# Four slot tiles of the two attention layers are summed in PSUM, in two places chosen by a number, behind a branch

## The chip, the core and the metric

The kernel runs on one core of one Trainium2 chip. The metric is device time in microseconds (us), from one launch; the median of the runs is compared. Engines are called PE (matrix multiply), DVE (vector), ACT (scalar), POOL (gpsimd) and SP (sync). POOL here does little but issue indirect DMAs, which gather table rows by a list of indices; SP issues the plain DMAs.

## What is computed

A stack of four graph layers over 3,125 nodes of 256 features and 50,000 edges, each followed by a residual and a layer norm. Edges come sorted by their destination `dst`; their density falls with the node number (`dst` is 3125 times a squared uniform number), so the first nodes have many edges and the last have few. Layers 1 and 2 are the ones that the change touches. Both are attention over the edges into a node:

```python
# layer 1: H = 4 heads of 64; layer 2: H = 8 heads of 64
score = <key of source, query of destination>        # layer 1
score = leaky(s_src[src] + s_tgt[dst])               # layer 2
m     = segment_max(score, dst);  ex = exp(score - m[dst])
out   = segment_sum(ex * value[src], dst) / segment_sum(ex, dst)
x     = layernorm(x + f(out))
```

Layer 0 is an edge-weighted mean with a gate, layer 3 a relational convolution. They are not changed.

## The kernel before

**Slot tiles.** Nodes are cut into 25 node tiles of 128. The sorted edges are cut into slot tiles of up to 128 edges that all go to one node tile; there are 416 (`TT`), so a node tile has between about 5 and 80 consecutive slot tiles. The number of the node tile of each slot tile is computed on the chip in `bucket` and kept in `tnode` (L333); engines read it into registers with `node_of` (L534), which loads four numbers at a time (L523).

**The edge loop** (`edge_softmax`, L714) goes over 26 steps of 16 slot tiles (`S`), each step four groups of four (`G`). For a group, `score` (L1228 in layer 1, L1390 in layer 2) has POOL gather four tiles of 128 table rows (2 KB a row; L509) into one of seven buffers `gb`, has SP load the one-hot matrices `oh` and `oht` (L548), multiplies on PE the transposed one-hots by the destination's query (`pqe`, L1237) or by its score part (`pst`, L1398), and reduces to scores on DVE (L1242, L1243; L1403 to L1405). When the 16 tiles have scores, `softmax` (L607 to L680) runs a chain of small operations that switches between PE, DVE and ACT and ends in the weights `ex` (L666).

**`weigh`** (L682) then adds the weighted values of a group into the accumulator `acc`, which holds all 25 node tiles in SBUF. It multiplies the gathered values by `ex` into `r`: DVE does all but `on_act` of the heads in one instruction (L697), ACT does the last `on_act` heads with one instruction per head and slot tile (L701). `on_act` is 2 in layer 1 and 3 in layer 2. Then, for each of the four slot tiles, PE multiplies `r` by the one-hot (L706: one 128x260 float32 matmul in layer 1, two in layer 2) into a PSUM tile `pr` of its own, and DVE adds that tile to the place in `acc` that the tile's node number names (L711):

```python
for j in range(G):
    pr = ps.tile([P, H // HB, 512], F32, name="pr", bufs=3)
    for n in range(H // HB):
        nc.tensor.matmul(pr[:, n, :HB * F], oh[:, j, :], r[:, j, n*HB:(n+1)*HB, :], start=True, stop=True)
    node = self.node_of(nc.vector, t0 + j)
    a = acc[:, ds(node * (H * F), H * F)]
    nc.vector.tensor_add(a, a, pr[:, :, :HB * F])
```

A gather buffer is free again when both DVE's and ACT's part of `r` are made. The scores of a step and the weighing of the step before it are interleaved; each engine's order of instructions is fixed when the program is built, by a scheduler that sees the whole program, and each engine runs its own list in order.

**Around the edge loops.** Layer 1's loop stands between the making of its tables (L1194 and the puts of L501) and a finishing stage (L1252 on) that scales `acc`, applies a typed matmul and prepares layer 2's tables. The scheduler puts parts of the neighbours into the loops' ends: weights of the finishing stage (`al` L1253, `wh` L1328) are loaded, `al` is scaled (L1258) and the vectors `wa` are made (L1336, L1337) while layer 1's last groups are still added up. The memsets of layer 2's accumulator (L1384) run beside its first gathers. There is one branch in the kernel, at L280: a sort that is skipped when the edges come sorted.

Of the kernel before, what the change touches and what calls it, by code (L numbers as in the profile page):

```python
# [9 lines left out]
F32 = mybir.dt.float32  # L10
# [10 lines left out]
G = 4  # L21
# [12 lines left out]
class Net:  # L34
# [4 lines left out]
    def __init__(self, ctx, tc, n_nodes, n_edges):  # L39
# [19 lines left out]
        self.below = c.tile([P, P], F32, name="below")  # L59
        nc.vector.tensor_scalar(self.below, self.iota, self.pidx, None, op0=ALU.is_gt)  # L60
# [152 lines left out]
    def bucket(self, src, dst, type16, type8, weight, relations):  # L213
# [27 lines left out]

        with tc.tile_pool(name="bk", bufs=1, side="right") as b:
# [40 lines left out]
            with tc.tile_pool(name="bkw", bufs=1, side="right") as w, tc.tile_pool(name="bkp", bufs=1, space=PSUM) as ps:  # L283
# [49 lines left out]
                nc.vector.tensor_copy(self.tnode, tno[0:1, :])  # L333
                p = pick(lambda k: bdf[:, k, :], "pdst")
# [202 lines left out]

    def used(self, engine, inst):
        self.uses.setdefault(engine.engine, []).append(inst.ins)
# [142 lines left out]
    def weigh(self, w, ps, acc, ohb, ex, value, H, t0, on_act):  # L682
# [19 lines left out]
        yield  # L702
        for j in range(G):
# [10 lines left out]
    def edge_softmax(self, w, sm, ps, hand, acc, H, F, score, on_act):  # L714
# [3 lines left out]
        def done(steps):  # L718
            for _ in steps:
                pass  # L720
# [3 lines left out]
        for t0 in range(0, self.TT + S, S):  # L724
# [8 lines left out]
            for n in range(S // G):  # L733
                if not last:
                    held.append(score(t0 + n * G, sc[:, :, n * G:(n + 1) * G]))
                if before and (last or n < S // G - 1):
                    value, oh = before[n]
                    done(self.weigh(w, ps, acc, oh, ex, value, H, t0 - S + n * G, on_act))
# [3 lines left out]
            if before:  # L742
                value, oh = before[-1]
                rest = self.weigh(w, ps, acc, oh, ex, value, H, t0 - G, on_act)
# [360 lines left out]
    def layer1(self, k_lin, q_lin, v_lin, a_lin, rel_att, rel_msg, rel_pri, skip,  # L1105
# [13 lines left out]
        with ExitStack() as layer:  # L1119
# [6 lines left out]
            with ExitStack() as edges:  # L1126
# [98 lines left out]
                with tc.tile_pool(name="e1g", bufs=7) as gp, tc.tile_pool(name="e1", bufs=2) as w, \  # L1225
                        tc.tile_pool(name="e1o", bufs=4) as op, tc.tile_pool(name="e1s", bufs=3) as sm, \
                        tc.tile_pool(name="e1p", bufs=2, space=PSUM) as ps:
                    def score(g0, out):  # L1228
                        gb = gp.tile([P, G, 2 * D], F32, name="gb1")
                        for j in range(G):  # L1230
                            self.gather(gb[:, j, :], table, self.s_rel, g0 + j)
                        oh, oht = self.onehots_back(w, op, g0)
                        pq = ps.tile([P, G, D], F32, name="pqe", bufs=2)
                        for j in range(G):
                            node = self.node_of(nc.tensor, g0 + j)
                            for n in range(3):
                                last = nc.tensor.matmul(pq[:, j, :], oht[:, j, :],  # L1237
                                                        q_all[:, ds(node * (3 * D) + n * D, D)],
                                                        start=n == 0, stop=n == 2)
                            self.used(nc.tensor, last)  # L1240
                        pd = w.tile([P, G, D], F32, name="pd")
                        nc.vector.tensor_mul(pd, gb[:, :, 0:D], pq)  # L1242
                        nc.vector.tensor_reduce(out.rearrange("p h t -> p t h"),  # L1243
                                                pd.rearrange("p j (h d) -> p j h d", h=H),
                                                axis=AX.X, op=ALU.add)
                        return gb[:, :, D:], oh

                    self.edge_softmax(w, sm, ps, hand, acc, H, F, score, 2)
# [125 lines left out]
    def layer2(self, Wo, bo, nxt):  # L1374
# [5 lines left out]
        with ExitStack() as layer:  # L1380
# [6 lines left out]
            with tc.tile_pool(name="e2g", bufs=7) as gp, tc.tile_pool(name="e2", bufs=2) as w, \  # L1387
                    tc.tile_pool(name="e2o", bufs=4) as op, tc.tile_pool(name="e2s", bufs=3) as sm, \
                    tc.tile_pool(name="e2p", bufs=2, space=PSUM) as ps:
                def score(g0, out):  # L1390
                    gb = gp.tile([P, G, HO + H], F32, name="gb2")
                    for j in range(G):
                        self.gather(gb[:, j, :], table, self.s_src, g0 + j)
                    oh, oht = self.onehots_back(w, op, g0)
                    pst = ps.tile([P, G, 3, H], F32, name="pst", bufs=1)
                    for j in range(G):
                        node = self.node_of(nc.tensor, g0 + j)
                        last = nc.tensor.matmul(pst[:, j, :, :], oht[:, j, :], s_tgt[:, ds(node * (3 * H), 3 * H)],  # L1398
                                                start=True, stop=True)
                        self.used(nc.tensor, last)  # L1400

                    pl = sm.tile([P, G, H], F32, name="pl")
                    nc.vector.tensor_reduce(pl, pst.rearrange("p j n h -> p j h n"), axis=AX.X, op=ALU.add)  # L1403
                    nc.vector.tensor_add(pl, pl, gb[:, :, HO:])
# [220 lines left out]
```

## Time and profile before

| what | us |
|---|---|
| median of 3 runs | 3369.55 (3362.56 to 3373.93) |
| the profiled execution's own time | 3362.08 |
| its span, first to last instruction | 3360.3 |
| layer 1's edge loop with its tail, 1168 to 1806 us of the span | 638 |
| layer 2's edge loop with its tail, 1968 to 2661 us of the span | 693 |

In the whole span PE is busy 80%, DVE 68%, POOL 54%, ACT 43%; in the two edge loops the shares differ, and they are read there. In the rows "busy, mean ns" is the time of a group of like instructions and the mean of one; "idle before, releaser" is how long the engine had stood still just before them, and who ended that. A float32 matmul is two passes in the records, so L706 counts two for each matmul. "issue" is time in which an engine waited for nothing that the profile shows. Rows that end in q (POOLq, DVEq, PEldq) are an engine's sequencer: branches, register loads, semaphores.

### The profile page before, as it was taken

What the parts mean: (1) busy time and instruction counts of PE and PEld (TensorE: products, weight loads), DVE (VectorE), ACT (ScalarE), POOL (GpSimd) and SP (SyncE); (2) the same over time, 40 slices, a digit from 0 to 9 for tenths busy, and PEclk for the clock granted to TensorE, in tenths of its full rate; (3) what the DMA queues carried; (4) which work ended last, traced back from release to release, by engine and by line L of the source; (5) the groups of instructions that cost most, each with busy time, mean ns of one, the idle gap of its engine ahead of it and who ended that gap; (6) DMA issues with size and microseconds to landing.
All of it is one profiled execution on the core that took longest, in us unless ns stands there. A gap on an engine that the chain in (4) does not pass through costs nothing. (4 is left out here: it accounts for less than half of the span.)

```text
span 3360.3 us, 50557 instructions
## 1 busy us (share of the span) xinstructions
PE 2693.6 (80%) x12679; PEld 1753.9 (52%) x12679; DVE 2274.4 (68%) x6046; ACT 1446.9 (43%) x4376; POOL 1827.1 (54%) x1850
## 2 busy tenths in 40 slices
PE   2779999999979777777775847888888887888885
PEld 1357777775545345555553525666666663333332
DVE  2646666676655378988886437888888873555556
ACT  1427777774456335544543215656656562000000
POOL 4037767771044167666662556676766202777773
PEclk9889999999989878888887878888888985565656
DMA  7249988884067877777774367878777235333332
GB/s 167 72 147 295 295 284 289 287 291 137 32 252 288 311 225 244 232 230 238 228 229 136 116 206 201 225 225 227 228 226 228 76 140 215 105 105 106 106 105 86
DMA packets 240616, 658.40 MB, mean 196 GB/s; under 512 B 47960, under 2 KB 87012, under 8 KB 234013
## 3 DMA queue, kind: packets, MB, share of 16 engines
q0 software_dynamic: 132400, 484.37, 46.4%
q1 hardware_dynamic: 104262, 167.53, 15.1%
q10 hardware_dynamic: 3676, 3.23, 0.5%
q8 instruction: 122, 2.00, 0.2%
q14 instruction: 156, 1.28, 0.1%
HBM read 513.06 MB, written 151.58 MB: 198 GB/s over the span
## 5 line engine op out<-in xcount | busy, mean ns | idle before, releaser
L509 POOL DMA_INDIRECT gb<-table,s_src x832 | 852.4, 1025 | 374.8 <-issue 203.9
L706 PE MATMUL pr<-r,oh 128*128 128x260 f32 x2496 | 733.6, 440 | 80.7 <-DVE acc L711 32.9
L706 PEld LDWEIGHTS pr<-r,oh 128*128 128x128 f32 x2496 | 502.5, 217 | 216.0 <-issue 33.1
L1509 POOL DMA_INDIRECT ring<-table,b_rel x391 | 369.9, 946 | 312.8 <-DVE oh L1519 194.0
L701 ACT ACTIVATE r<-gb,ex 128x64 f32<-128x64 f32 x2080 | 522.4, 336 | 0.0
L509 POOL DMA_INDIRECT gb<-table,s_rel x416 | 405.4, 974 | 204.9 <-issue 106.0
L711 DVE TENSOR_TENSOR acc<-acc,pr 128x260 f32 (+1 forms) x832 | 457.7, 550 | 72.7 <-PE pr L706 60.8
L1538 PE MATMUL pa<-ring,oh 128*128 x832 | 428.9, 628 | 84.1 <-DMA ring<-table,b_rel 41.2
L1538 PEld LDWEIGHTS pa<-ring,oh 128*128 128x128 f32 x832 | 193.7, 283 | 319.6 <-DVE oh L1519 215.2
L1545 DVE TENSOR_TENSOR x<-x,pa 128x256 f32 x416 | 175.2, 421 | 227.0 <-PE pa L1538 225.2
L1237 PE MATMUL pqe<-q_all,oht 128*128 x1248 | 207.8, 306 | 91.9 <-DVE pd L1242 76.1
L693 ACT CAST oh<-ohb 128x512 f32<-128x512 bf16 x208 | 128.3, 618 | 307.2 <-PE pr L706 278.6
L589 ACT ACTIVATE r<-mv,eps 128x4 f32<-128x4 f32 (+3 forms) x27 | 7.9, 297 | 536.5 <-DVE mv L575 533.1
L697 DVE TENSOR_TENSOR r<-gb,ex 128x512 f32<-128x512 f32 (+1 forms) x208 | 225.8, 1086 | 12.9 <-ACT ex L666 9.2
L979 PE MATMUL pa<-gb,ohw 128*128 128x272 f32 x832 | 223.7, 402 | 5.3 <-DVE acc L981 3.8
L1237 PEld LDWEIGHTS <-oht 128*128 128x128 bf16 x1248 | 131.6, 107 | 126.8 <-issue 86.0
L961 PE MATMUL pre<-xb,oht 128*128 x1248 | 193.7, 273 | 0.0
L981 DVE TENSOR_TENSOR acc<-acc,pa 128x272 f32 x416 | 180.7, 434 | 6.2 <-PE pa L979 3.4
L928 DVE TENSOR_TENSOR places<-iota,s_dl 128x512 bf16<-128x512 f32 x104 | 72.0, 692 | 161.5 <-ACT ohw L976 161.5
L956 PE MATMUL pre<-gb,idb 128*128 128x512 bf16 x624 | 169.3, 381 | 5.3 <-DMA gb<-table,s_src 5.3
L979 PEld LDWEIGHTS pa<-gb,ohw 128*128 128x128 f32 x832 | 141.5, 190 | 55.6 <-issue 35.1
L967 DVE SCALAR_TENSOR_TENSOR hg<-hg,aw 128x256 f32<-128x256 f32 x416 | 159.4, 421 | 16.1 <-ACT hg L965 16.1
(381 smaller groups left out, 4291.6 us busy)
## 6 DMA issues: line engine op xcount, KB each, us to landing
ohb<-oh_d SPq DMA_DIRECT2D x104, 256.0 KB
oht<-oht_d SPq DMA_DIRECT2D x104, 256.0 KB
table<-row SPq DMA_DIRECT2D x25, 1024.0 KB
gb<-table,s_src POOLq DMA_INDIRECT x832, 4.5
oh_d<-places SPq DMA_DIRECT2D x52, 256.0 KB
oht_d<-oht SPq DMA_DIRECT2D x52, 256.0 KB
sgm<-seg SPq DMA_DIRECT2D x26, 320.0 KB
gb<-table,s_rel POOLq DMA_INDIRECT x416, 4.4
```

What stands on the lines that cost most here:

```text
L509: self.nc.gpsimd.indirect_dma_start(out=out, out_offset=None, in_=table, in_offset=bass.IndirectOffsetOnAxis(ap=idx[:, t:t + 1], axis=0))
L697: nc.vector.tensor_mul(r[:, :, :nd, :hw], v[:, :, :nd, :], ex[:, :nd, s0:s0 + G].rearrange("p h t -> p t h")[:, :, :, None].to_broadcast([ ...
L701: nc.scalar.activation(r[:, j, h, :hw], v[:, j, h, :], AF.Copy, scale=ex[:, h, s0 + j:s0 + j + 1])
L706: nc.tensor.matmul(pr[:, n, :HB * F], oh[:, j, :], r[:, j, n * HB:(n + 1) * HB, :].rearrange("p h f -> p (h f)"), start=True, stop=True)
L711: self.used(nc.vector, nc.vector.tensor_add(a, a, pr[:, :, :HB * F]))
L961: last = nc.tensor.matmul(q, oht[:, 0, j, :], xbr[:, ds(node * (3 * D) + n * D, D)], start=False, stop=False)
L979: nc.tensor.matmul(pa, ohw[:, j, :], gb[:, j, 0:ET + D], start=True, stop=True)
L981: self.used(nc.vector, nc.vector.tensor_add(a, a, pa))
L1237: last = nc.tensor.matmul(pq[:, j, :], oht[:, j, :], q_all[:, ds(node * (3 * D) + n * D, D)], start=n == 0, stop=n == 2)
L1509: st = nc.gpsimd.indirect_dma_start(out=ring[:, at:at + D], out_offset=None, in_=table, in_offset=bass.IndirectOffsetOnAxis(ap=b_rel[:, b: ...
L1538: last = nc.tensor.matmul(pa, oh[:, j, :], ring[:, ds(at, D)], start=True, stop=True)
L1545: self.used(nc.vector, nc.vector.tensor_add(a, a, pa))
```

## The change

- In `bucket`, DVE computes for each group whether its two middle slot tiles go to another node tile than the first (`bank`: 0 or 512) and counts in `odd` the middle tiles that go to neither the first's nor the last's node tile. Seven small DVE operations.
- Each edge loop is built twice, behind a branch on `odd`: all five engines load `odd` into a register and compare. If it is over 0 the old way runs, otherwise the new one (`quick`).
- In `quick`, `weigh` takes a PSUM tile of two banks for a group and for each four heads. The first slot tile is summed into bank 0, the last into bank 1, each with `start`; the two middle ones are accumulated at an offset that PE reads from `bank`. Two matmuls with one row of zeros end the two sums. DVE then adds bank 0 at the first tile's node and bank 1 at the last tile's node.
- `on_act` becomes 1 in layer 1 and 2 in layer 2 in `quick`.
- In both ways layer 1's `pqe` is made in halves of two slot tiles with three buffers instead of whole groups with two, so L1242 becomes two instructions of 128x512.
- `below`, used only at the start, moves to a pool that is given up early.

```diff
+                t4 = tno[0:1, :].rearrange("p (g j) -> p g j", j=G)
+                away = w.tile([1, 2, TT // G, G - 2], F32, name="away")
+                for n, j in enumerate((0, G - 1)):
+                    nc.vector.tensor_tensor(away[:, n], t4[:, :, 1:G - 1],
+                                            t4[:, :, j:j + 1].to_broadcast([1, TT // G, G - 2]), op=ALU.not_equal)
+                nc.vector.tensor_scalar(self.bank, away[:, 0], 512.0, None, op0=ALU.mult)
+                nc.vector.tensor_mul(away[:, 0], away[:, 0], away[:, 1])
+                odd = w.tile([1, 1], F32, name="odd")
+                nc.vector.tensor_reduce(odd, away[:, 0], axis=AX.XY, op=ALU.add)
+                nc.vector.tensor_copy(self.odd, odd)
...
+    def bank_of(self, engine, t):
+        key = engine.engine, "bank"
+        g = t // (2 * G)
+        if self.numbers.get(key, (None, None))[0] != g:
...
+                return self.nc.values_load_multi_w_load_instructions(
+                    self.bank[0:1, 2 * g:2 * g + 2, :].rearrange("p g j -> p (g j)"), engines=[engine.engine], min_val=0, max_val=512,
...
+    def two_ways(self, run):
+        odd = self.nc.values_load(self.odd[0:1, 0:1], min_val=0, max_val=self.TT,
...
+        with self.tc.If(odd > 0) as cmp:
+            fresh(False)
+        with cmp.Else():
+            fresh(True)
...
+        if quick:
+            for n in range(H // HB):
+                pr = ps.tile([P, 2, 512], F32, name="pr", bufs=H // HB + 1)
+                for j in (0, G - 1, *range(1, G - 1)):
+                    if j in (0, G - 1):
+                        o = pr[:, min(j, 1), :HB * F]
+                    else:
+                        o = pr.rearrange("p b f -> p (b f)")[:, ds(self.bank_of(nc.tensor, t0 + j), HB * F)]
+                    last = nc.tensor.matmul(o, oh[:, j, :], r[:, j, n * HB:(n + 1) * HB, :].rearrange("p h f -> p (h f)"),
+                                            start=j in (0, G - 1), stop=False)
+                self.used(nc.tensor, last)
+                for b in range(2):
+                    nc.tensor.matmul(pr[:, b, 0:1], self.idb[0:1, :], self.idb[0:1, 1:2], start=False, stop=True)
+                yield
+                for b, j in enumerate((0, G - 1)):
+                    node = self.node_of(nc.vector, t0 + j)
+                    a = acc[:, ds(node * (H * F) + n * HB * F, HB * F)]
+                    self.used(nc.vector, nc.vector.tensor_add(a, a, pr[:, b, :HB * F]))
+                    yield
+            return
...
-                        pq = ps.tile([P, G, D], F32, name="pqe", bufs=2)
-                        for j in range(G):
...
+                            for j0 in range(0, G, 2):
+                                pq = ps.tile([P, 2, D], F32, name="pqe", bufs=3)
...
+                                nc.vector.tensor_mul(pd[:, j0:j0 + 2], gb[:, j0:j0 + 2, 0:D], pq)
...
-                    self.edge_softmax(w, sm, ps, hand, acc, H, F, score, 2)
+                        self.edge_softmax(w, sm, ps, hand, acc, H, F, score, 1 if quick else 2, quick)
+                self.two_ways(along)
...
-                self.edge_softmax(w, sm, ps, hand, acc, H, F, score, 3)
+                    self.edge_softmax(w, sm, ps, hand, acc, H, F, score, 2 if quick else 3, quick)
+            self.two_ways(along)
```

## The prediction

> **What bounds the kernel now.** I read first the windows view, which gives each engine's busy time by stage, because the change touches only the two edge loops. These are a steady stretch of layer 1 and one of layer 2 (start:end, length, then busy us and instructions of PE, PE's weight loads, DVE, ACT and POOL, the granted clock, the DMA share and GB/s).
>
> ```profile
> 1430.00:1540.00 110.00, 83.36 (x426) 58.16 (x427) 95.83 (x203) 54.79 (x212) 73.41 (x75) 0.84 0.75 233
> 2260.00:2370.00 110.00, 90.83 (x406) 67.84 (x406) 94.53 (x209) 65.17 (x253) 77.14 (x73) 0.89 0.79 226
> ```
>
> DVE is busy 87% and 86%, PE 76% and 83%: no engine is full, and several are near it. So I read the groups of instructions inside layer 1 (1210 to 1770) and then inside layer 2 (2040 to 2590), shapes apart, and the waits of POOL in each.
>
> ```profile
> L509 POOL DMA_INDIRECT gb<-table,s_rel x387 | 377.9, 976 | 188.8 <-issue 90.1 <-ACT r L701 80.0 <-DVE acc L711 8.2
> L701 ACT ACTIVATE r<-gb,ex 128x64 f32<-128x64 f32 x780 | 198.8, 336 | 0.0
> L711 DVE TENSOR_TENSOR acc<-acc,pr 128x260 f32 x386 | 160.9, 417 | 33.3 <-PE pr L706 28.1 <-issue 1.9
> L1242 DVE TENSOR_TENSOR pd<-gb,pqe 128x1024 f32<-128x1024 f32 x95 | 115.3, 1214 | 7.8 <-DMA gb<-table,s_rel 7.5
> L697 DVE TENSOR_TENSOR r<-gb,ex 128x512 f32<-128x512 f32 x95 | 65.2, 686 | 0.3 <-PE pr L706 0.3
> ```
>
> ```profile
> L509 POOL DMA_INDIRECT gb<-table,s_src x349 | 376.7, 1079 | 175.1 <-issue 84.7 <-ACT r L694 77.3 <-DMA gb<-table,s_src 6.1
> L711 DVE TENSOR_TENSOR acc<-acc,pr 128x520 f32 x352 | 240.2, 682 | 25.6 <-PE pr L706 21.5 <-DVE hand L638 0.3
> L697 DVE TENSOR_TENSOR r<-gb,ex 128x1280 f32<-128x1280 f32 x88 | 130.8, 1486 | 8.3 <-ACT ex L666 7.6 <-PE pr L706 0.3
> ```
>
> A step is 16 gathers. Layer 1 makes 387 in 560 us, 23.15 us a step; layer 2 makes 349 in 550 us, 25.2 us. POOL needs 0.30 us between gathers whatever happens (the "issue" idle). So 16 gathers cost it 16 x (0.976 + 0.30) = 20.4 us in layer 1 and 16 x (1.079 + 0.30) = 22.1 us in layer 2. The rest, 2.7 and 3.1 us a step, it waits, mostly for a gather buffer (80.0 and 77.3 us): the buffer is free when r is made, r needs ex, and ex needs the scores of the next gathers. The timeline of layer 2 shows the ring: ex at 2321.45, ACT's part of r done at 2324.94, the gather behind it at 2325.21, its group's last score at 2335.25, next ex near 2346.5. So both loops are rings of latency just above POOL's own floor. A shorter ring gains at most 2.7 and 3.1 us of 23 and 25.
>
> **The change, part by part.** First: which way runs? The new way needs that no group touches three node tiles. Then a node tile would have to have one or two slot tiles; with the reference's density the last one has about 430 edges and the next-thinnest over 1,000, so four or more each. It is taken.
>
> *ACT, removed.* One head fewer is four ACT instructions a group; in throughput one costs 198.8/780 = 0.255 us, so r's ACT part ends 1.0 us earlier. In layer 1 the buffer is freed by that part (releaser L701), in layer 2 too by the timeline. DVE's part grows but stays the shorter. Worth 1.0 us of the ring in both layers.
>
> *DVE, removed and added, a step.* Layer 1: 16 adds become 8, -8 x 0.417 = -3.34. L697 grows by 256 elements; from 0.686 at 512 to 1.486 at 1280 an element costs 1.04 ns, so +0.267 a group, +1.07. L1242 becomes two of 512 elements, nearest row L697 at 0.686: +0.16 a group, +0.63. Sum -1.64. Layer 2: still 16 adds, of 260 instead of 520 elements: 16 x (0.682 - 0.417) = -4.24, and +1.07: -3.17. What lies between a step's scores and its ex counts on the ring: in layer 2 the timeline shows 9 of 16 adds there (2311.3 to 2320.8), 9 x 0.265 = 2.4 us; in layer 1 I take half of the 1.64, 0.8 us.
>
> *PE, added.* Two matmuls a group (layer 1) or four (layer 2) that end the sums: 8 and 16 a step, 624 in all. No such row exists before; the nearest is layer 2's small bf16 pair:
>
> ```profile
> L1398 PEld LDWEIGHTS <-oht x344: 94/98/152, 2052.4 to 2586.2; 128*128 128x128 bf16 x172
> L1398 PE MATMUL pst<-s_tgt,oht x344: 172/175/228, 2052.6 to 2586.3; 128*128 x172
> ```
>
> Four such loads stand in 0.37 us of the timeline, 0.093 each, the low end; 0.175, the whole of a matmul, is the high end (min/median/max in the rows). I take 0.12, near the low end, because in a row of matmuls the loads overlap. The Trainium skill would make it cheaper: "TensorE: Matmul & The Clock Gate", section Part 1, says that matmuls follow each other at 25 ns however short they are. By that all 624 cost 16 us; by the row, which has the weight load in it, 75. The row decides. So +1.0 us a step in layer 1 and +1.9 in layer 2. The offsets cost one register load for two groups, 0.33 us by the register loads that PE has (L523), two a step: nothing where the two matmuls ahead of it in the built order cover it, 0.7 us a step if not; their address operations (46 ns, as L1398 has) go ahead of the array. I put half of all this on the ring: 0.5 us in layer 1, 1.2 in layer 2, where PE then needs 20.8 + 1.9 + 0.7 = 23.4 us a step.
>
> *POOL, slowed.* Gathers that meet L697 take 1.19 to 1.25 us in the timeline instead of 0.95, and the mean excess over 0.946 is 0.03 us in layer 1 (0.69 us multiplies) and 0.13 in layer 2 (1.49). A longer L697 makes more of them long: at most its whole lengthening, 0.267 x 4 = 1.07 us a step, at least nothing. The skill's "SBUF — State Buffer", section Who interferes with whom, says of this pair that a `tensor_tensor` with both inputs in SBUF contends only with what gpsimd reads, and that the making of descriptors needs the write side: by that rule +0. The trace has the excess exactly at L697, so I take +0.5 and +1.0: POOL's floor becomes 20.9 and 23.1.
>
> *The rings.* Layer 1: -1.0 (ACT) - 0.8 (DVE) + 0.5 (PE) = -1.3, within the 2.2 that POOL's floor leaves: 23.15 - 1.3 is 21.8. Layer 2: -1.0 - 2.4 + 1.2 = -2.2, but POOL stands at 23.1 and PE at 23.4, and a loop that meets two limits at once reaches neither; I take 23.9, that is -1.3. Times 26 steps: -34 and -34 us.
>
> *The borders.* The branch's price is seen once, at L280.
>
> ```profile
> L280 POOLq EVENT_SEMAPHORE  x5: 17/42/43, 89.7 to 92.8; - x5
> L280 POOLq COMPARE_BRANCH  x1: 53/53/53, 82.0 to 82.0; - x1
> L280 DVEq COMPARE_BRANCH  x1: 72/72/72, 145.6 to 145.6; - x1
> L280 DVEq EVENT_SEMAPHORE  x1: 21/21/21, 148.4 to 148.4; - x1
> ```
>
> DVE goes on 2.8 us after it jumped, POOL 7.7 us. "Runtime: NRT & Kernel Launch", Instruction fetch mechanics, has the reason and no price: a jump out of the two pages held makes the engine wait for a fetch. By the rule every engine pays at each far jump, ten here; by the rows it counts only where nothing covers it. With the load of `odd` (0.5 to 0.7 us at L278):
> - into layer 1: POOL waits 7.6 us for the last put to land (1160.7 to 1168.27). The jump hides there; uncovered it would cost 8. I take +2 (0 to 6).
> - out of layer 1: the built order puts the scaling of `al` (4 x 0.47) and the making of `wa` (8 x 0.69 less overlap) on DVE behind the branch and ahead of the reciprocal that the finishing stage starts with. Before, they ran inside the loop's tail, where DVE waits for PE. That is 7.2 us, plus a wait for `al`, `wh` and `sk`, which SP and ACT now fetch behind their own branches (before: issued at 1772, used at 1787), plus DVE's jump of 1 to 3, less 2 to 3 that DVE's freed tail gives back. +9 (4 to 16). Behind DVE wait the `xad` stores, then POOL's gathers (1821), then all.
> - into layer 2: the last put ends at 1966.2 and the first gather starts at 1968.25, so only 2 us of POOL's 8.3 hide, and the ring starts with 16 gathers in a row. +7 (2 to 10). DVE's memsets stay ahead of the branch; its 3 us hide, since the first scores are whole only at 1993.
> - out of layer 2: `wo` loads after the loop in both kernels and covers the jump. +2 (0 to 3).
> - `bucket`: seven DVE operations of 0.15 to 0.4 us, while DVE waits there for PE's picks. +1 (0 to 3).
>
> Sum +21 (6 to 38). Half-size `pqe` buffers: same three-halves look-ahead, at nothing; PE waited 67 us for L1242 before, which a stall would show.
>
> *The sum*, against the profiled execution: 3362.1 - 34 - 34 + 21 = 3315. The median of the runs lies 7.5 above that execution, so 3323; I say 3322.
>
> **The rivals.**
>
> *Both rings fall to POOL's floor* (all waits for buffers go): -2.2 x 26 = -57 and -2.1 x 26 = -55, borders +21: -91, near 3280. For it: DVE loses a seventh of its work in layer 2. Against: softmax's handovers between three engines stay.
>
> *PE becomes layer 2's bound: slower.* PE loads the next weights under a running matmul. Under a matmul of one column nothing hides, so each pair of end matmuls may cost 2 x 0.175 and lay bare the next float32 load (0.19): 0.54 a pair, 4.3 us a step, and PE needs 20.8 + 4.3 + 0.7 = 25.8 us, besides the 2.0 us a step in which it waits for softmax (L664 for DVE, 44.0 us in 22 steps): about 27. Layer 2 then loses 1.8 x 26 = 47 us; layer 1, where PE is at 17.5 + 2.2 + 0.7 = 20.4, keeps -20; borders +21: +48, near 3417. It decides from about 0.46 us a pair. For it: PE is already at 83% in layer 2 and layer 2's chain that ended last has L706 as its largest part. Against: part of PE's busy time is at a lowered clock (0.88 on average), which denser work may raise.
>
> *The gain is given back at the borders*: they cost 38, the rings give 18 each or less: 3365 to 3375.
>
> *The old way runs* after all: borders +21, split L1242 +0.63 x 26 = +16: near 3406.
>
> **How the numbers follow.** Forecast 0.52 (its own range 3295 to 3355), POOL's floor 0.17, PE's bound 0.18, given back 0.11, old way 0.02. A measurement of this kernel can tell about 0.3%, 10 us, from no change. Faster: 0.52 + 0.17 less 0.02 at the edge, 0.67. Same: 0.09. Slower: 0.18 + 0.02 + 0.04, 0.24. The range leaves out the lower half of POOL's floor and part of PE's bound: 3268 to 3407.
>
> **What would show it.** ACT's L701 groups halve and drop by a third; L711 has 208 + 416 instructions of 128x260; gathers wait less than 2 us a step for r; from first gather to last add layer 1's loop takes near 606 us and layer 2's near 666. Wrong: PE over 90% busy in layer 2 with DVE waiting for it (the second rival); a gather mean over 1.15 us; more than 40 us between layer 1's last add and the gathers of `xa`.

## The result and the profile after

The changed kernel takes 3410.9 us, the kernel before on the same chip 3368.7: a ratio of 1.0126 (95% interval 1.0108 to 1.0144), slower by 42 us. The forecast was 3322 with faster at 0.67, and the time lies outside the range of 3268 to 3407. The profiled execution takes 3416.7 us (span 3414.6, before 3360.3), so the traces have 54.3 us to explain. The changed kernel's four executions took 3405.1, 3405.2, 3416.7 and, at a granted clock of 0.55 instead of 0.84, 4478.2 us, and six later runs (first runs of four kernels and the last two below) fell in a time when the kernel before itself took 4045 to 4050 us, so that of those only ratios are used. Cut at the first and last gathers and adds of each loop, they lie here:

| stretch | before, us | after, us | difference | predicted |
|---|---|---|---|---|
| start to layer 1's first gather | 1168.3 | 1169.5 | +1.2 | +2 |
| layer 1, first to last gather | 601.7 | 650.8 | **+49.1** | -34 |
| last gather to the gathers of `xa` | 51.0 | 52.5 | +1.5 | +9 |
| `xa` to layer 2's first gather | 147.2 | 145.9 | -1.3 | +7 |
| layer 2, first to last gather | 660.5 | 660.6 | +0.1 | -34 |
| layer 2, last gather to the end of the last add | 38.0 | 39.2 | +1.2 | (in the loop) |
| last add to the end | 693.5 | 696.2 | +2.7 | +2 |

(Layer 2's loop with its tail ends at 2667 us in the kernel before, not at 2661 as the table of the kernel before has it.) Layer 1's loop is the loss, and layer 2's gain is absent. The borders and the branch, which I had priced at +21, come to 1.2 + 1.5 - 1.3 + 2.7 = +4. The windows view of the changed kernel (columns as in the prediction; both stretches lie as before within the loops, the second 50 us later):

```profile
1430.00:1540.00 110.00, 85.69 (x424) 56.84 (x423) 81.66 (x163) 34.30 (x129) 65.73 (x68) 0.82 0.67 206
2310.00:2420.00 110.00, 94.64 (x466) 68.63 (x465) 81.59 (x211) 50.14 (x192) 82.17 (x70) 0.89 0.80 225
```

DVE and ACT did lose work: DVE falls from 96 and 95 us of 110 to 82. The loops did not follow. In layer 1 POOL issues 68 gathers where it issued 75. The groups inside layer 1 (1210 to 1820), shapes apart, and below them those inside layer 2 (2090 to 2640):

```profile
L521 POOL DMA_INDIRECT gb<-table,s_rel x387 | 376.9, 974 | 238.1 <-ACT r L751 126.3 <-issue 88.0 <-ACT r L744 7.5
L1315 DVE TENSOR_TENSOR pd<-gb,pqe 128x512 f32<-128x512 f32 x190 | 126.4, 675 | 4.2 <-DMA gb<-table,s_rel 2.4 <-PE pr L766 1.8
...
L751 ACT ACTIVATE r<-gb,ex 128x64 f32<-128x64 f32 x384 | 104.2, 337 | 0.0
...
L747 DVE TENSOR_TENSOR r<-gb,ex 128x768 f32<-128x768 f32 x97 | 92.6, 954 | 2.4 <-issue 2.0 <-ACT ex L715 0.4
...
L771 DVE TENSOR_TENSOR acc<-acc,pr 128x260 f32 x193 | 81.2, 421 | 98.7 <-PE pr L766 98.3
...
L728 DVE TENSOR_TENSOR acc<-acc,fac 128x260 f32 x24 | 10.3, 428 | 35.6 <-ACT fac L725 35.6
```

```profile
L521 POOL DMA_INDIRECT gb<-table,s_src x348 | 412.2, 1185 | 144.5 <-issue 75.6 <-ACT r L751 38.0 <-ACT r L744 11.8
...
L747 DVE TENSOR_TENSOR r<-gb,ex 128x1536 f32<-128x1536 f32 x88 | 154.6, 1757 | 29.1 <-PE pr L761 18.4 <-PE pr L766 9.5
L771 DVE TENSOR_TENSOR acc<-acc,pr 128x260 f32 x349 | 145.7, 418 | 47.0 <-PE pr L766 31.7 <-DVE acc L771 5.4 <-DVE smA L676 4.0
```

The counts are as predicted: half the adds in layer 1, narrower ones in layer 2, L747 at 0.95 and 1.76 us. New are three waits. In layer 1 each step now waits 126.3/24 = 5.3 us for the gather buffer (before 80.0/24 = 3.3), DVE waits 98.3 us for the end of PE's sums (before 28.1), and the rescaling of `acc` (L728, L679 before) waits 35.6 us for ACT (before 15.8). In layer 2 a gather takes 1.185 us on average, over the 1.15 that I had named as a sign that the forecast is wrong.

Each step of layer 1 now looks like this. Rows of the changed kernel's timeline around one `ex`:

```profile
1454.76 0.22 ACT L715 ACTIVATE ex<-mis 128x64 f32<-128x64 f32 x1 [3.31 <-PE mis L713]
...
1456.24 0.43 DVE L728 TENSOR_TENSOR acc<-acc,fac 128x260 f32 x1 [1.76 <-ACT fac L725]
1456.59 0.95 DVE L747 TENSOR_TENSOR r<-gb,ex 128x768 f32<-128x768 f32 x1
...
1458.28 0.94 POOL L521 DMA_INDIRECT gb<-table,s_rel  x1 [5.37 <-ACT r L751]
```

`ex` is there at 1454.98, but DVE's next instruction in its queue is the rescaling, which needs ACT's `fac` and stands 1.76 us. Only then comes the first `r`. POOL's gather starts at 1458.28, 0.74 us after L747 ends. In the steps before and after this one the distance is 0.75 and 0.74. ACT's part of that `r` had ended at 1456.91 already, so it is DVE's part that frees the buffer, although the row names ACT. In the kernel before the same two DVE instructions come in both orders, in alternate steps. Its DVE timeline in one step and in the next:

```profile
1435.20 0.43 DVE L679 TENSOR_TENSOR acc<-acc,fac 128x260 f32 x1 [1.25 <-ACT fac L676]
1435.54 1.21 DVE L1242 TENSOR_TENSOR pd<-gb,pqe 128x1024 f32<-128x1024 f32 x1
1436.67 0.69 DVE L697 TENSOR_TENSOR r<-gb,ex 128x512 f32<-128x512 f32 x1
...
1461.02 0.67 DVE L697 TENSOR_TENSOR r<-gb,ex 128x512 f32<-128x512 f32 x1
...
1461.78 0.43 DVE L679 TENSOR_TENSOR acc<-acc,fac 128x260 f32 x1
```

The first step (rescaling ahead of `r`, and L1242 between them) takes 26.2 us from `ex` to `ex`, the second (`r` ahead) 20.7. The mean of 23.15 us a step that I worked with was the mean of two different steps. The changed kernel's steps are all long, 25.2 and 26.0 us in turn, though in its order nothing stands between the rescaling and `r`.

### The profile page after: what moved, and what is told of

Read it like the earlier page. It is cut to its first block, busy times and chain, and to the rows that moved or that the text cites. A ratio compares the mean times of both kernels' runs of the same rounds, so it can differ in the third digit from the quotient of the medians.

```text
span 3414.6 us, 50986 instructions
## 1 busy us (share of the span) xinstructions
PE 2790.6 (82%) x13303; PEld 1790.0 (52%) x13303; DVE 2167.5 (63%) x5948; ACT 1249.0 (37%) x3543; POOL 1871.4 (55%) x1850
## 5 line engine op out<-in xcount | busy, mean ns | idle before, releaser
L521 POOL DMA_INDIRECT gb<-table,s_src x832 | 897.8, 1079 | 328.1 <-issue 195.4
L761 PEld LDWEIGHTS pr<-r,oh 128*128 128x128 f32 x2496 | 515.8, 219 | 192.4 <-ACT r L751 47.1
L521 POOL DMA_INDIRECT gb<-table,s_rel x416 | 404.4, 972 | 253.1 <-ACT r L751 126.3
L771 DVE TENSOR_TENSOR acc<-acc,pr 128x260 f32 x624 | 261.3, 419 | 165.5 <-PE pr L766 146.1
L751 ACT ACTIVATE r<-gb,ex 128x64 f32<-128x64 f32 x1248 | 324.3, 336 | 0.0
L747 DVE TENSOR_TENSOR r<-gb,ex 128x768 f32<-128x768 f32 (+1 forms) x208 | 281.8, 1355 | 40.5 <-PE pr L761 24.5
L1311 PE MATMUL pqe<-q_all,oht 128*128 x1248 | 223.0, 301 | 89.3 <-DVE pd L1315 33.2
L1311 PEld LDWEIGHTS <-oht 128*128 128x128 bf16 x1248 | 120.8, 103 | 136.8 <-issue 54.2
```

Of the source, the lines that this page charges most:

```text
L521: self.nc.gpsimd.indirect_dma_start(out=out, out_offset=None, in_=table, in_offset=bass.IndirectOffsetOnAxis(ap=idx[:, t:t + 1], axis=0))
L747: nc.vector.tensor_mul(r[:, :, :nd, :hw], v[:, :, :nd, :], ex[:, :nd, s0:s0 + G].rearrange("p h t -> p t h")[:, :, :, None].to_broadcast([ ...
L751: nc.scalar.activation(r[:, j, h, :hw], v[:, j, h, :], AF.Copy, scale=ex[:, h, s0 + j:s0 + j + 1])
L761: last = nc.tensor.matmul(o, oh[:, j, :], r[:, j, n * HB:(n + 1) * HB, :].rearrange("p h f -> p (h f)"), start=j in (0, G - 1), stop=False)
L771: self.used(nc.vector, nc.vector.tensor_add(a, a, pr[:, b, :HB * F]))
L1311: last = nc.tensor.matmul(pq[:, j - j0, :], oht[:, j, :], q_all[:, ds(node * (3 * D) + n * D, D)], start=n == 0, stop=n == 2)
```

## The experiments

Theory 1, formed from the trace after: an add cannot start before all four slot tiles of its group are summed, and DVE's queue stands behind it. Its rivals: 2, the branch and the borders; 3, the half-size `pqe` buffers; 4, the end matmuls and register loads on PE; 5, the head moved from ACT to DVE. Theory 6, that the order in DVE's queue has changed, came last. "Loop" is first to last gather from here on.

**Without the branch, and one layer at a time.** `self.two_ways(along)` becomes:

```diff
-                self.two_ways(along)
+                along(True)
```

> The changed kernel with the new way alone in both layers: no load of `odd`, no branch, no old way. Theory 1 (the loss is inside layer 1's loop: an add can't start before the sum of all four slot tiles is ended, and DVE's queue stands behind that add): layer 1's loop stays at the changed kernel's 651 us from first to last gather, only the border steps fall, so 5 to 10 us less than the changed kernel, near 3402. Theory 2 (branch, far jumps and lost overlap at the borders make the loss): near the kernel before, 3369, or below it.

Measured: 3433.3 us, 1.0185 of before (1.0166 to 1.0203), slower than with the branch, which neither theory had. Layer 1's loop is 652.8, as theory 1 has it; theory 2 falls. For the new way in one layer alone the other call becomes `along(False)`; for layer 2 alone, layer 1 also keeps its whole `pqe` buffers.

> No branch; the new way in layer 1 alone, layer 2 in the old way with on_act 3. Theory 1: layer 1's loop at 651 us, 49 longer than before, so about 3415. Theory 2: near 3369. Theory 3 (half-size pqe buffers make layer 1's loss): about 3415 too, told apart by the kernel with the half-size buffers alone.

Measured: 3413.8 us, 1.0128 (1.0109 to 1.0146), layer 1's loop 654.0.

> No branch; the new way in layer 2 alone, layer 1 as before with whole pqe buffers and on_act 2. Theory 1: layer 2's loop took 660.5 us in both kernels, so 3364 to 3375, no difference that can be told. My prediction's part for layer 2 would give 3335.

Measured: 3390.5 us, 1.0060 (1.0041 to 1.0079), above theory 1's 3364 to 3375. Layer 2's loop is 673.1, not 660.6; its tail is 39.1 (before 38.0). So the new way costs about 43 us in layer 1 and 19 in layer 2, and these add up to the 62 of the kernel without branch. The changed kernel's layer 2 has a gain at its start that hides this: its first 104 gathers take 167.1 us, in the kernel before 174.1, without branch 186.2. SP's queue shows what goes with it. The loads of `x` stand behind four loads of one-hots in the changed kernel (first two rows) and behind two without branch (last two):

```profile
2036.74 0.31 SPq L597 DMA_DIRECT2D oht<-oht_d  x1
...
2037.80 20.84 SPq L1446 DMA_DIRECT2D x<-own  x5
```

```profile
2021.82 0.82 SPq L597 DMA_DIRECT2D oht<-oht_d  x2
...
2025.41 21.68 SPq L1446 DMA_DIRECT2D x<-own  x5
```

What that place is worth alone is measured further down.

**The half-size buffers alone**, in the kernel before:

```diff
-pq = ps.tile([P, G, D], F32, name="pqe", bufs=2)
+for j0 in range(0, G, 2):
+    pq = ps.tile([P, 2, D], F32, name="pqe", bufs=3)
...
+    nc.vector.tensor_mul(pd[:, j0:j0 + 2], gb[:, j0:j0 + 2, 0:D], pq)
```

> The kernel before with one edit: pqe in halves of two slot tiles with three buffers, so L1242 is two instructions of 128x512. Theory 1: DVE's extra 0.63 us a step at most, 0 to 16 us, so 3369 to 3385. Theory 3 (the half-size buffers make PE wait behind DVE, ahead of the transposition that ex needs): 30 to 50 us, 3400 to 3420.

Measured: 3397.4 us, 1.0078 (1.0059 to 1.0098); layer 1's loop 628.8. The +26 us lie between the two expectations: theory 1's upper end was 16, theory 3's lower end 30. With four buffers instead of three:

> The kernel before with pqe in halves of two slot tiles and four buffers: as much PSUM as the two whole buffers had, the same built order on DVE as with three. Against the half-size buffers with three (3397 us, layer 1's loop 629 us; before 602). If the loss is the missing fourth half (PE waits for DVE to give a half back), layer 1 falls to about 605. If it is the split L1242 and the order that the scheduler makes of it, it stays at 620 to 629.

Measured: 3397.8 us, 1.0099 (1.0064 to 1.0135), loop 633.1. The number of buffers isn't it. What has changed with the split is the order in DVE's queue: from the fifth step on the rescaling stands ahead of the first `r` in every step, with L1243 between them.

**The sums without end matmuls.** Without branch, tiles 0 and 1 are summed at a fixed place, 2 and 3 at the other. This leaves out the choice of the place, so a middle tile can be added to the wrong node:

```diff
-o = pr.rearrange("p b f -> p (b f)")[:, ds(self.bank_of(nc.tensor, t0 + j), HB * F)]
+o = pr[:, j // 2, :HB * F]
...
-for b in range(2):
-    nc.tensor.matmul(pr[:, b, 0:1], self.idb[0:1, :], self.idb[0:1, 1:2], start=False, stop=True)
```

> The changed kernel without branch, and in both layers without the end matmuls and the register loads of `bank`: slot tiles 0 and 1 of a group are summed into bank 0, 2 and 3 into bank 1, at fixed places, in the order 0, 3, 1, 2 with stop on the last two; a group whose middle tile belongs to the other bank's node is therefore added to the wrong node. To be held against the kernel without branch (3433 us; layer 1's loop 653 us, layer 2's 670). Theory 1 (the adds wait for all tiles of a group): both sums still end late, so layer 1 stays within 10 us of 653. Theory 4 (the end matmuls and register loads on PE are the loss in the sums): layer 1 falls to the 629 us of the half-size buffers alone, and layer 2 by 20 to 30.

Measured: 3368.5 us, 1.0018 (1.0002 to 1.0033). Layer 1's loop is 602.7, 50 less than without branch; layer 2's is 673.0 (without branch 670.3). Theory 4 foretold the direction in layer 1, not the size, and its fall in layer 2 did not come.

> As the kernel with fixed places, but the matmuls come in the order 0, 1, 3, 2, so that bank 0's sum is whole after two slot tiles; DVE's built order is the same. What is left out is the same. Theory 1: the first add of a group waits for two tiles fewer, 0.5 to 1 us a group less stall on DVE, so layer 1 20 to 40 us shorter than with the order 0, 3, 1, 2. Theory 4: no difference between the two orders.

Measured: 3373.9 us, 1.0034 (1.0014 to 1.0053), layer 1's loop 603.7. This run does not decide about theory 1, for the edit did not do what it was meant to. The first add still starts 2.03 us after the group's first matmul (1431.06 to 1433.09), when the whole row of 1.99 us is over, so it waits for the group's last matmul in either order.

**The heads.**

> The changed kernel without branch, with on_act 2 and 3 kept, so that no head goes from ACT to DVE. Against the kernel without branch (3433 us). Theory 5 (DVE's longer L747 delays the buffers' release and slows POOL's gathers): gathers of layer 2 back to a mean of 1.07 to 1.09 us from 1.17, layer 2 10 to 40 us shorter, layer 1 up to 15. Theory 1 alone: within 10 us of 3433.

Measured: 3537.3 us, 1.0515 (1.0477 to 1.0552). Layer 1's loop is 22 us shorter (630.7), but layer 2's takes 819.6, 149 more. Layer 2's gathers are faster (1.036 us, without branch 1.157), as theory 5 has it, and do not help. The waits of this kernel inside layer 2 (2150 to 2600; total us, times, longest):

```profile
POOL gb L521 <- ACT r L744: 149.8, 21, 12.1
ACT hand L688 <- DVE hand L687: 99.0, 14, 9.3
DVE pl L1480 <- DMA gb<-table,s_src: 78.8, 32, 5.1
```

In the order that the scheduler built here, DVE has two groups' scores (L1480) between the first operations of a softmax. DVE waits there for gathers that are still under way, and the softmax behind it, and POOL behind that, wait with it. So this run is about an order too, and says little of the heads. The heads alone, in the kernel before (`on_act` 1 and 2), were run twice, as were the next three kernels; of each first run only the ratio counts.

> The kernel before with on_act 1 and 2: one head of four or eight goes from ACT to DVE. My prediction: the ring 1.0 us shorter by ACT, DVE 1.07 us more a step, half of it on the ring, so 0 to 13 us less in each layer, 3345 to 3370. Theory 5: DVE's part of r ends later and frees the gather buffer later, and gathers that meet the longer L747 take longer: layer 1 5 to 20 us longer, layer 2 up to 30 longer.

> The kernel before with on_act 1 and 2, once more. On the chip where before takes 4045 us its ratio was 0.990, so the shift of a head helped there. My prediction's step (ACT's part of r frees the buffer): 3345 to 3370. Theory 5 (DVE's part frees it, and L697's length slows the gathers): 3375 to 3410.

Measured: 0.9905 (0.9870 to 0.9940), then 3393.2 us, 1.0089 (1.0067 to 1.0112). The sign differs; the second is the one to compare: +29 us. Layer 1's loop is 626.0, layer 2's 667.4, and layer 2's 416 gathers take 1.135 us on average, against 1.067. In layer 1 the rescaling now stands ahead of `r` in every step, and still the steps alternate. DVE's queue behind `ex` in a step of 26 us and in the next, of 23 us:

```profile
1445.22 0.43 DVE L679 TENSOR_TENSOR acc<-acc,fac 128x260 f32 x1 [1.55 <-ACT fac L676]
1445.57 1.21 DVE L1242 TENSOR_TENSOR pd<-gb,pqe 128x1024 f32<-128x1024 f32 x1
1446.70 0.95 DVE L697 TENSOR_TENSOR r<-gb,ex 128x768 f32<-128x768 f32 x1
...
1471.16 0.43 DVE L679 TENSOR_TENSOR acc<-acc,fac 128x260 f32 x1 [0.40 <-ACT fac L676]
1471.51 1.21 DVE L1243 TENSOR_REDUCE sc<-pd 128x16 f32<-128x1024 f32 x1
1472.64 0.95 DVE L697 TENSOR_TENSOR r<-gb,ex 128x768 f32<-128x768 f32 x1
```

`r` comes 2.5 us after `ex` in both. What differs is L1242, which gives PE a `pqe` buffer back: where it stands behind the rescaling, PE waits for it.

```profile
1446.84 1.86 PE L1237 MATMUL pqe<-q_all,oht 128*128 x8 [1.86 <-DVE pd L1242]
```

In the kernel before it is the same: PE stands 5.1 us ahead of its `pqe` matmuls in each long step, where L1242 stands behind the rescaling, and 0.9 in each short one. So L1242's place is a rival to the rescaling's place there, and no run parts the two.

**The end matmuls.** First with the sums at fixed places (the kernel above with its two end matmuls put back), then in the kernel before, where they end nothing:

```diff
 nc.tensor.matmul(pr[:, n, :HB * F], oh[:, j, :],
...
+if j == G - 1:
+    for b in range(2):
+        nc.tensor.matmul(pr[:, n, 300 + b:301 + b], self.idb[0:1, :], self.idb[0:1, 1:2], start=True, stop=True)
```

> The changed kernel without branch, sums at fixed places (slot tiles 0 and 1 into bank 0, 2 and 3 into bank 1, so a middle tile can be added to the wrong node), no register loads of `bank`, but with the end matmuls. DVE's built order is that of the kernel with neither (3368 us, layer 1's loop 603 us), but for one place. If the end matmuls themselves cost layer 1 its 50 us: near 3425, loop about 645. If the register loads and the order that the scheduler makes with them cost it: near 3375, loop 603 to 612.

> The kernel with sums at fixed places and end matmuls, without register loads of `bank` and without branch, once more, since the first run fell on a chip on which the kernel before takes 4045 us (a middle tile can be added to the wrong node, as there). If the end matmuls themselves cost layer 1 its 50 us: near 3425, layer 1's loop about 645. If the register loads and the order that the scheduler makes with them cost it: near 3375, loop 603 to 612. On the slow chip its ratio to before was 0.995, which speaks for the second.

> The kernel before, and in each group of both layers the small matmuls of the change (two for each four heads) with nothing to end: they write unused columns of the last slot tile's PSUM bank. DVE's built order is that of before. My prediction's price of 0.12 us each with half on the ring is 1.5 us a step, 20 to 40 us: near 3395. If a pair costs the 0.2 us that PE's records show but lies beside other work: within 10 us of before.

> The kernel before with the small matmuls of the change and nothing to end, once more. On the chip where before takes 4045 us its ratio was 1.040. If that is their price in any order of the work, 3369 x 1.04 = 3503; by my prediction's price, near 3395; if they lie beside other work, within 10 us of before.

Measured at fixed places: 0.9948 (0.9915 to 0.9981), then 3445.9 us, 1.0254 (1.0232 to 1.0276): neither number that was expected. Layer 1's loop is 618.0, so the ends take 15 us of its 50 and the register loads with their order 35; layer 2's is 725.0, 52 more than without ends, in yet another order. In the kernel before: 1.0399 (1.0317 to 1.0480), then 3383.1 us, 1.0054 (1.0032 to 1.0076), with DVE's order unchanged. That is the clean price: 18 us for 624 small matmuls; in the profiled execution 4 lie in layer 1's loop, 15 in layer 2's and 3 in its tail.

**The loads of `x`.** In the kernel before, PE stands once for long at layer 2's start. The waits of 1985 to 2012:

```profile
DVE pl L1403 <- PE pst L1398: 15.4, 2, 15.2
PE pst L1398 <- DMA oht<-oht_d: 14.9, 1, 14.9
```

The one-hots of the second step lie in SP's queue behind loads of `x`. The edit puts these loads behind the last one-hots loaded until then (`self.loaded`), which the trace shows to be the second step's, not the third's as expected below:

```diff
-                with self.tc.issue_after(self.uses[nc.vector.engine][-1]):
+                with self.tc.issue_after(self.loaded):
                     while self.later:
```

> The kernel before with one edit: the five loads of `x` (L1371) go into SP's queue behind the one-hot loads of layer 2's third step, not ahead of those of the second. In the kernel before PE stands 14.9 us in layer 2's first softmax because the one-hots of the second step lie behind 2.6 MB of `x`. If that stall is on the path, 8 to 12 us less than before, near 3356; if POOL's gathers set the start anyway, no change.

> The kernel before with the loads of `x` behind the one-hot loads of layer 2's third step, once more. If PE's 14.9 us in layer 2's first softmax are on the path: 8 to 12 us less than before, near 3356. On the chip where before takes 4045 us there was no difference.

Measured: 1.0010 (0.9981 to 1.0040) in the first run, then **3346.8 us against 3364.2, 0.9951 (0.9935 to 0.9966)**: faster than both kernels. The wait is gone from the list, and the first 104 gathers take 160.3 us (before 174.1), layer 2's loop 651.0 (660.5). The profiled execution itself was the slowest of its six, 3362.8 us.

**The order of rescaling and `r`.** The rescaling is issued behind the first `r` of a step (`made` is that multiplication):

```diff
+        if self.rescale:
+            with self.tc.issue_after(made.ins):
+                self.rescale()
+            self.rescale = None
```

> The changed kernel, branch and all, with one edit: the rescaling of the accumulator (L728), which waits for ACT's `fac`, is put behind the first multiplication of `r` (L747) in DVE's queue, where in the changed kernel it stands ahead of it in every step of layer 1. Theory 6 (in layer 1 `r` is late because L728 holds up DVE's queue for ACT's `fac`, and POOL waits for DVE's part of `r`): `r` comes 1.5 us earlier in each of 26 steps, layer 1's loop falls from 651 us to about 612, the whole to about 3372. Theory 7 (the register loads of `bank` themselves hold PE up): layer 1 stays at 640 to 651 and the whole at about 3405.

> The kernel before with two edits of order and nothing of the change: L679 behind the first L697 of a step, and the loads of `x` behind the one-hots of layer 2's third step (which alone gave 17 us). Theory 6: in before, layer 1's steps alternate between 21 us, where L697 stands ahead of L679, and 25.7, where L679 and L1242 stand ahead; with all steps in the first order layer 1's loop falls from 602 to about 555 and the whole to about 3305. If the alternation has another cause (PE's granted clock, or POOL's floor): layer 1 stays near 600 and the whole near 3350.

Measured: 1.0095 (1.0070 to 1.0121) and 0.9969 (0.9943 to 0.9996), both against a before of 4050 us. Layer 1's loop is 849.5 and 841.0 there. The first run of the kernel with the `x` loads alone, whose layer 1 is that of before, has 848.1. Neither expectation can be held against this: steps of 33 us stand on something else. In that first run PE's weight loads for `r` stand 147 us in 21 such steps (1430 to 2130) for nothing that the profile shows, in before 15 us in 24 steps. So theory 6 was not tested where it counts. What can be compared speaks against it as the whole cause: that first run still alternates, 31.3 us with `r` ahead and 34.7 with the rescaling ahead, mean 33.0, and with `r` ahead in every step the steps are 32.7. The alternation went and the mean stayed.

## Why the prediction was wrong, by its steps

The mean of each step's parts in layer 1 (steps 5 to 24 of each trace), parted by what DVE has behind `ex`, up to `r`. All times run from start to start; a softmax starts with DVE's first operation on the scores (`smA`).

| kernel | behind `ex`, ahead of `r` | `ex` to `r`, us | `ex` to next softmax | softmax to `ex` | step |
|---|---|---|---|---|---|
| before, 10 steps | nothing | 0.5 | 15.3 | 5.6 | 21.0 |
| before, 10 steps | rescaling, L1242 | 2.5 | 18.9 | 6.8 | 25.8 |
| changed | rescaling | 1.8 | 19.1 | 6.5 | 25.6 |
| before, half-size `pqe` | rescaling, L1243 | 2.5 | 18.2 | 6.2 | 24.4 |
| before, heads moved, 10 steps | rescaling, L1242 | 2.5 | 20.1 | 5.9 | 26.0 |
| before, heads moved, 10 steps | rescaling, L1243 | 2.5 | 17.2 | 5.7 | 22.9 |
| before, end matmuls, 10 steps | nothing | 0.5 | 15.2 | 5.6 | 20.8 |
| before, end matmuls, 10 steps | rescaling, L1242 | 2.5 | 19.1 | 6.9 | 26.0 |
| fixed places, no ends | nothing | 0.3 | 16.6 | 6.7 | 23.3 |
| fixed places, ends | nothing | 0.3 | 16.4 | 7.5 | 23.9 |

Where `r` is first, the next softmax starts 15 to 17 us after `ex`, otherwise 17 to 20. In the kernel with the heads kept (not in the table) the two orders give equal steps of 24.4, and with the heads moved two orders that both have the rescaling first give 26.0 and 22.9. So the rescaling's place goes with the long steps in most kernels, but it does not by itself set the step.

- **The frame of the whole sum failed**: "Layer 1: -1.0 (ACT) - 0.8 (DVE) + 0.5 (PE) = -1.3". It adds durations to a step of 23.15 us and takes the order in each queue as given. The scheduler built another order. Two edits that I had priced at nothing or as a gain, the half-size buffers and the moved head, each take layer 1's steps of 21 us away when made alone (+27 and +24 us of loop), and the changed kernel has none left. That 27 and 24 add up to about its 49 is no proof: the kernel with fixed places and no ends has both edits too, `r` first, and a loop of 602.7. Between it and the kernel without branch lie the end matmuls (15 us) and the register loads with the order built around them (35).
- **Half-size `pqe` buffers "at nothing"**: measured +26 us. I looked for the cost in PE's waits for a buffer; four buffers instead of three did not bring it back (loop 633.1 against 628.8).
- **"ACT, removed ... Worth 1.0 us of the ring in both layers"**: in the kernel before, ACT's part of `r` frees the buffer in the step where `r` is first (it ends at 1463.41, the gather starts at 1463.67). In the other, DVE's does (1437.36, gather at 1438.10), as in the changed kernel, and the moved head makes that part longer. With the head moved alone the gather starts 0.74 us behind DVE's part in both kinds of step (12 steps in a row), so DVE's part frees the buffer in both. The head alone cost 29 us.
- **DVE's saving** is real as busy time (20.3 us a step before, 459.0/610 x 25.2 = 19.0 after) and is offset by the wait for whole sums (98.3 us in layer 1's window). The latter is theory 1; that it costs time of its own is argued from comparing rows of one order (23.3 against 21.0 us a step), not shown. The chain of releasers speaks for both: followed back from one `ex` to the last, all 20 steps of the changed kernel go through `fac`, the first `r` behind it and then that group's whole sum; sums of `r` stand for 9.5 of its 25.6 us a step, in the kernel before for 5.0 of 23.4. Such a chain shows what was waited for, not what a step would take without it.
- **PE, 0.12 us for each end matmul**: 18 us for 624 is 0.03 us each. (My half on the ring was also added up wrongly: half of 1.0 + 0.7 and of 1.9 + 0.7 is 0.85 and 1.3, not 0.5 and 1.2.) The rows of L766 in both loops are as the nearest row said, and a pair takes 0.20 us in the timeline:

```profile
L766 PEld LDWEIGHTS <-idb x574: 89/93/113, 1213.3 to 2638.9; 1*128 1x128 bf16 x192
L766 PE MATMUL pr<-idb x574: 157/166/183, 1213.3 to 2638.9; 1*128 1x1 bf16 x192
```

That is what a matmul shows, not what it takes from the path. The estimate of 16 us from the Trainium skill's 25 ns ("TensorE: Matmul & The Clock Gate", Part 1) came nearer, though most of the work may only have lain beside other work. The second rival, PE as layer 2's bound, is not what happened: PE is 86% busy in the window above. Its 3417 lies near the measured time by luck, as the loss is in layer 1; its own sum, 25.8 + 2.0, is 27.8 and not about 27.
- **POOL slowed, +1.0 us a step in layer 2**: undersized. 16 x (1.185 + 0.30) = 23.8 us is POOL's floor in layer 2 now, not 23.1: it rose by 1.7, over the 1.07 that I had called the most. A step of 550/348 x 16 = 25.3 us leaves 1.5 us of waiting above that floor where I had left 0.8. My "1.19 to 1.25 us" for a gather that meets L697 came from one stretch; over layer 2 of the kernel before such gathers take 1.29 us on average and up to 2.29. The Trainium skill's "SBUF — State Buffer", section Who interferes with whom, read as +0 for this pair, does not fit: 1.067 us a gather before, 1.135 with the head moved and nothing else. The same section says that a DVE instruction with two SBUF inputs contends with a GpSimd instruction that reads SBUF, and the gathers take their indices from SBUF; this sentence is not contradicted, and no run shows which part of a gather waits.
- **Borders +21**: measured +4, and without the branch the kernel is slower by about 20 us (the ratios 1.0185 and 1.0126). In the traces 10 us of that lie in layer 2's loop: its first 104 gathers take 19 us longer (186.2 against 167.1), where the loads of `x` stand ahead of the second step's one-hots, and the rest 9 less. POOL's jump is hidden into layer 2 as into layer 1. POOL's last put and first gather of layer 2, in the kernel before and then in the changed one:

```profile
1965.21 0.97 POOL L501 DMA_INDIRECT table<-row,n_put  x1 [0.30 <-issue]
1968.25 0.98 POOL L509 DMA_INDIRECT gb<-table,s_src  x1 [2.06 <-DMA table<-row,n_put]
```

```profile
2015.38 0.97 POOL L513 DMA_INDIRECT table<-row,n_put  x1 [0.30 <-issue]
2018.68 0.98 POOL L521 DMA_INDIRECT gb<-table,s_src  x1 [2.32 <-DMA table<-row,n_put]
```

The price of 7.7 us from L280 was not met here: the gather waits 2.32 us where it waited 2.06. PE's own record of the branch into layer 1 is long, and covered, since PE then waits for its first `oht` until 1171.76:

```profile
L582 PEldq COMPARE_BRANCH  x1: 6514/6514/6514, 1161.0 to 1161.0; - x1
```

So the step that failed is shown: durations were added to an order that was no longer there, and two edits priced at nothing and at a gain of 1.0 us a step cost 26 and 29 us each when made alone. What stays open is what in the new order sets a step: the rescaling's place, L1242's place or the wait for whole sums, and how much of the 35 us between fixed and read places is the register loads themselves. In layer 2 the lengthened gathers are shown; what else took the gain is not.

## What to carry to other kernels

When a scheduler orders the queues, price a change from the order that it builds, not from the old order plus durations: list, for the few instructions behind each handover (here those behind `ex`), what now stands ahead of them, and whom that waits for. Look at the single steps before taking a mean step: where steps with the same work alternate between 21 and 26 us, look at the order first. And look for a single long wait at a loop's start: five loads moved behind others gave 17 us here.

## What the runs showed of the hardware

PE's granted clock falls to half once in nearly every step of layer 1 (25 times in the loop's 26 steps), and PE has little to do just before, in the softmax. The windows view of the changed kernel across one step:

```profile
1450.00:1453.00 3.00, 1.30 (x10) 0.88 (x10) 3.00 (x13) 0.57 (x3) 2.30 (x3) 0.98 0.81 225
1454.00:1458.00 4.00, 2.64 (x10) 1.41 (x9) 2.24 (x4) 2.65 (x12) 0.00 (x0) 0.50 0.53 176
1458.00:1462.00 4.00, 4.00 (x13) 2.62 (x13) 1.93 (x4) 0.47 (x1) 2.83 (x3) 0.50 0.42 98
1466.00:1470.00 4.00, 3.47 (x19) 2.26 (x19) 2.82 (x5) 0.53 (x3) 3.11 (x3) 1.00 0.88 295
```

PE's timeline has the price: the first group's sum takes 3.81 us (1457.69) and a later one 1.99 (1467.80). In steps 5 to 24 the first sum takes 3.56 to 3.81 us. The kernel before has the same clock (0.50 from 1462 to 1466), but there DVE's first add waits for one slot tile at that clock, and here for four.

The second surprise is a gather that meets a long DVE multiplication:

```profile
2329.54 1.75 DVE L747 TENSOR_TENSOR r<-gb,ex 128x1536 f32<-128x1536 f32 x1
2329.90 2.21 POOL L521 DMA_INDIRECT gb<-table,s_src  x1 [0.30 <-DVE pl L1480]
...
2333.67 0.95 POOL L521 DMA_INDIRECT gb<-table,s_src  x1 [0.30 <-issue]
```

The two lie beside each other for 1.39 us, and the gather is 1.26 us longer than the later one. Of layer 2's 416 gathers 139 meet such a multiplication; they take 1.60 us on average and up to 2.46, the others 0.95.
